# Layer 0 of a two-layer macaron block: where the side chains' matmuls may stand in the TensorE queue, and which engines do two of their elementwise steps

## The chip, the cores and the metric

The kernel runs on one core of a Trainium2 chip. A core has five engines that run side by side, each through its own queue in order: PE (TensorE, matmuls; its weight loads are shown as PEld), DVE (VectorE), ACT (ScalarE), POOL (GpSimd) and SP (SyncE, which here issues most DMAs). The metric is the device time of one execution in microseconds; the time before is a median of 3630.62 us over three runs (3627.19 to 3651.11).

## What is computed

The input x is 16 batches of 512 tokens of 128 channels. Two layers follow one another; each adds to x half of a feed-forward block, an attention, and half of the same feed-forward block again. The change touches layer 0 alone. Cut to that layer:

```python
def fp4_linear(x, w):                 # blocks of 16 along the last dimension
    return einsum('bsk,nk->bsn', fp4_quant_dequant(x), fp4_quant_dequant(w))

def L0_ffn(x, w_gate, w_up, w_down):  # 128 -> 352 -> 128
    h = silu(fp4_linear(x, w_gate)) * fp4_linear(x, w_up)
    return fp4_linear(h, w_down)

def L0_attn(x, ...):                  # 16 heads of 8 channels
    dist = clip(idx[None, :] - idx[:, None], -64, 64) + 64
    pe_k, pe_v = rel_emb_k[dist], rel_emb_v[dist]
    q, k, v = split(x @ W_qkv + b_qkv);  q = q / sqrt(8)
    score = einsum('bhqd,bhkd->bhqk', q, k) + einsum('bhqd,qkd->bhqk', q, pe_k)
    attn = softmax(score)
    ctx = einsum('bhqk,bhkd->bhqd', attn, v) + einsum('bhqk,qkd->bhqd', attn, pe_v)
    return ctx @ W_out + b_out

x = x + 0.5 * L0_ffn(layernorm(x), ...)
x = x + L0_attn(layernorm(x), ...)
x = x + 0.5 * L0_ffn(layernorm(x), ...)
```

Layer 1 has a linear attention and a feed-forward block with its own small attention and a mixture of experts; its code is the same before and after.

## The kernel before

Layer 0 works in units: one batch and one half of its queries (256 of 512), so 32 units. The code of a unit consists of several generators, and `interleave` (L446) steps them in turn, each by its own schedule: a generator gets a number of steps and a span of positions in units, and the one that is furthest behind its schedule makes its next step. The order in which instructions are written this way is called the order of emission here. It is a priority, not yet the order of execution: a scheduler places each instruction on its engine's queue at compile time, by its own estimate of when the operands and buffers are ready, and may place a later one first. `issue_after(ins)` around some instructions forbids that towards one instruction: those on the same engine as `ins` are queued behind it, without a wait.

The generators of the loop (`layer0`, L457) are:

- The stream of maxima (`maxima`, L332), for a later unit: 32 score groups. A score group (`scores`, L257) is four matmuls of 128 columns (L263) and, within the band of relative positions, eight of 64 (L267), into one PSUM bank of the pool `pS` ("sps", three banks). DVE takes the row maxima out of the bank (L341), and at the end the maxima are reduced (L347), transposed on PE (L349) and sent through DRAM into the operand BD.
- `main` (L358): the same 32 score groups again; ACT takes the exponentials out of the bank (L369). Behind each eight groups stand bursts of small matmuls (L272, L274) for attn times v ("av") and attn times the band table ("rps"). The band part is written to DRAM and read back as `cr`; av is copied to `cx` by ACT (L412).
- `fin` (L416): adds cr to cx on DVE (L422, two instructions), transposes cx (L430), divides by the sum (L433, L434), transposes (L437, copied out in L438) and multiplies by W_out (L440), and adds the result to x (L443). Its span is the stretch from 0.45 to 0.9 of the next unit.
- `prep` (L275) and `prepV` (L316): the layer norm and projection of a later batch (L282, L286, L305, L319).
- `head` and `tail`: `FFN.half` (L107) before and after the attention, for 256 tokens each. It normalizes, quantizes (`quant_steps`, L64, with POOL at L79 and L81), transposes (L115), makes "gate" (L121, tanh at L122, L123) and "up" (L125), multiplies both on DVE straight from PSUM (L126), quantizes the product h, transposes it (L133, copied in L135 and L136), multiplies by w_down (L139) and adds to x (L140). `head` loads x (L475) first; `tail` stores it last.

The matmuls of `fin`, `prep`, `prepV`, `head` and `tail` are called chain matmuls here. They share the PSUM pool `pM` ("mps") with two banks, and each bank is free again when the instruction that reads it out is done. `head` and `tail` share the pool `fk` with two buffers for each name; "q_y" is one of the names. Before the loop, head, prep and maxima of the first units are written out one after the other (L510 to L517): head(0), prep(0), maxima(0,0), then head(1), prep(1), 14 steps of the next maxima, and head(2).

The number of steps that each generator is given in `layer0` stands beside it: 33 per unit for the maxima, 59 for `main`, 5 for `fin`, 21 for `head` and `tail`, 11 for `prep`.

Of the kernel before, what the change touches and what calls it, by code (L numbers as in the profile page):

```python
# [25 lines left out]
class K:  # L26
# [23 lines left out]
    def ln_steps(s, xb, out, wk, n):  # L50

        nc=s.nc
        st=wk.tile([128,n,6],F32,name="ln_st"); mv=wk.tile([128,n,2],F32,name="ln_mv")
        for j in range(n):
            nc.vector.bn_stats(st[:,j,:],xb[:,j,:])  # L55
            nc.vector.bn_aggr(mv[:,j,:],st[:,j,:]); yield  # L56
        ve=wk.tile([128,n],F32,name="ln_ve"); rs=wk.tile([128,n],F32,name="ln_rs"); mr=wk.tile([128,n],F32,name="ln_mr")
        nc.vector.tensor_scalar(ve,mv[:,:,1],1e-5,None,ALU.add)  # L58
        nc.gpsimd.tensor_tensor(rs,ve,s.negh[:,:n],ALU.pow); yield  # L59
        nc.vector.scalar_tensor_tensor(mr,mv[:,:,0],-1.0,rs,ALU.mult,ALU.mult)  # L60
        for j in range(n):
            nc.scalar.activation(out[:,j,:],xb[:,j,:],AF.Identity,bias=mr[:,j:j+1],scale=rs[:,j:j+1])  # L62
        yield
    def quant_steps(s, X, wk, P, nb, tag):  # L64

        nc=s.nc
        n=nb*16
# [3 lines left out]
        nc.vector.tensor_scalar(sc[:P],sc[:P],float(np.float32(1/6)),1e-12,ALU.mult,ALU.max)  # L71
# [6 lines left out]
        nc.vector.scalar_tensor_tensor(y[:P],y[:P],SHRINK,M[:P],ALU.mult,ALU.add); yield  # L78
        nc.gpsimd.tensor_tensor(M[:P],y[:P],M[:P],ALU.subtract)  # L79
        M3=M.rearrange("p (b k) -> p b k",k=16)  # L80
        nc.gpsimd.tensor_tensor(M3[:P],M3[:P],sc[:P].unsqueeze(2).to_broadcast([P,nb,16]),ALU.mult)  # L81
        yield M

class FFN:
# [22 lines left out]
    def half(f, xb, half, wk, pp):  # L107

        s=f.s; nc=s.nc
        xh=xb[:,2*half:2*half+2,:]  # L110
        xn=wk.tile([128,2,128],F32,name="f_x")
        yield from s.ln_steps(xh,xn,wk,2)
        for xq in s.quant_steps(xn.rearrange("p a b -> p (a b)"),wk,128,16,"xq"): yield
        ps=pp.tile([128,512],F32,name="mps")
        for j in range(2): nc.tensor.transpose(ps[:,j*128:(j+1)*128],xq[:,j*128:(j+1)*128],s.ident)  # L115
        xqT=wk.tile([128,256],F32,name="f_x"); nc.scalar.copy(xqT,ps[:,:256]); yield
        h=wk.tile([128,2,I],F32,name="f_h")
        for j in range(2):
            t=h[:,j,:]
            g=pp.tile([128,512],F32,name="mps")  # L120
            nc.tensor.matmul(g[:,:I],xqT[:,j*128:(j+1)*128],f.wguT[:,0,:],start=True,stop=True)  # L121
# [3 lines left out]
            nc.tensor.matmul(u[:,:I],xqT[:,j*128:(j+1)*128],f.wguT[:,1,:],start=True,stop=True)  # L125
            nc.vector.scalar_tensor_tensor(t,u[:,:I],0.5,t,ALU.mult,ALU.mult); yield  # L126
        for hq in s.quant_steps(h.rearrange("p a b -> p (a b)"),wk,128,44,"hq"): yield
        hq=hq.rearrange("p (a b) -> p a b",a=2)
        for j in range(2):
            ps=pp.tile([128,512],F32,name="mps")  # L130
            for c in range(3):
                P=min(128,I-c*128)
                nc.tensor.transpose(ps[:P,c*128:(c+1)*128],hq[:,j,c*128:c*128+P],s.ident)  # L133
            hT=wk.tile([128,3,128],F32,name="hT",bufs=1)
            nc.scalar.copy(hT[:,0:2,:],ps[:,:256])  # L135
            nc.scalar.copy(hT[:96,2,:],ps[:96,256:384])  # L136
            for c in range(3):
                P=min(128,I-c*128)
# [7 lines left out]
class Attn0:  # L146
# [110 lines left out]
    def scores(a, out, kt, half, b, BD, TQ, KS):  # L257
# [2 lines left out]
        sd=a.side(kt,blk); ib=a.inband(kt,blk)  # L260
        o4=out.rearrange("p (x g c) -> p g x c",x=8,g=4)
        for g in range(4):
            nc.tensor.matmul(o4[:,g],KS[:,sd,g*512+kt*128:g*512+(kt+1)*128],BD[:,g,:,b*32:b*32+32].rearrange("p h (x j) -> p x h j",j=4),start=(g==0),stop=(not ib and g==3),skip_group_check=True)  # L263
        if ib:
            for x in range(8):
                w0=kt*128-blk*32-x+a.OFF
                nc.tensor.matmul(out[:,x*64:x*64+64],a.ET[:,w0:w0+128],TQ[:,:,b*32+4*x:b*32+4*x+4],start=False,stop=(x==7),skip_group_check=True)  # L267

    xnT={}; pend={}; last=None
    def run(a, mms):  # L270
# [4 lines left out]
    def prep(a, b, xb, wk, pM):  # L275
# [6 lines left out]
        for j in range(4): nc.tensor.transpose(ps[:,j*128:(j+1)*128],xn[:,j,:],a.ident)  # L282
        xnT=a.xnT[b]=wk.tile([128,512],F32,name="xnT",bufs=2); nc.scalar.copy(xnT,ps); yield
        for z in range(2):
            ps=pM.tile([128,512],F32,name="mps")
            nc.tensor.matmul(ps,a.w[:,z*128:(z+1)*128],xnT,start=True,stop=True)  # L286
# [18 lines left out]
        nc.tensor.matmul(ps[:32],a.eb.rearrange("p a b -> p (a b)"),q,start=True,stop=True)  # L305
# [26 lines left out]
    def maxima(a, b, half, wk, pS, pM):  # L332
# [16 lines left out]
        nc.tensor.transpose(ps[:,:128],mk.rearrange("p s b x -> p (s b x)"),a.ident)  # L349
# [66 lines left out]
    def fin(a, b, half, X, wk, pM):  # L416

        s=a.s; nc=a.nc; cx,cr=a.pend.pop((b,half)); xb=X[b]
        def add():
            for s2 in range(2):  # L420
                o=cx.rearrange("p z (b j s x) -> p s (z b) x j",j=4,s=2,x=4)[:,s2]
                nc.vector.tensor_tensor(o,o,cr.rearrange("p (x j z b s) -> p s (z b) x j",x=4,j=4,z=4,s=2)[:,s2],ALU.add)  # L422
        if a.last is None: add()
        else:
            with s.tc.issue_after(a.last): add()
        yield
        cn=wk.tile([128,2,128],F32,name="cn")
        for t in range(2):
            ps=pM.tile([128,512],F32,name="mps")
            for z in range(4): nc.tensor.transpose(ps[:,z*128:z*128+128],cx[:,z,t*128:t*128+128],a.ident)  # L430
# [6 lines left out]
        for t in range(2): nc.tensor.transpose(ps[:,t*128:t*128+128],cn[:,t,:],a.ident)  # L437
        ct=wk.tile([128,2,128],F32,name="cn").rearrange("p a b -> p (a b)"); nc.scalar.copy(ct,ps[:,:256])  # L438
        ps=pM.tile([128,512],F32,name="mps")
        for t in range(2): nc.tensor.matmul(ps[:,t*128:(t+1)*128],ct[:,t*128:(t+1)*128],a.wo,start=True,stop=True)  # L440
# [16 lines left out]
def layer0(tc, s, w, src, dst, nb=16):  # L457
# [3 lines left out]
    with ExitStack() as c:  # L461
# [576 lines left out]
```

## Time and profile before

| | |
|---|---|
| median of three runs | 3630.62 us |
| the profiled execution's own time | 3633.94 us |
| its span, first to last instruction | 3632.2 us |
| mean granted TensorE clock | 0.900 |
| PE busy | 2825.0 us, 78% of the span |
| PEld busy | 2032.3 us, 56% |
| DVE busy | 2444.9 us, 67% |
| ACT busy | 1693.8 us, 47% |
| POOL busy | 838.9 us, 23% |
| L341, maxima out of PSUM, x1024 | 702.5 us, 701 ns each |
| L369, exponentials out of PSUM, x1024 | 576.4 us, 599 ns each |
| L263, scores, x8192 | 736.4 us of PE |
| L267, band scores, x7168 | 370.3 us of PE |

The profile is of one execution, taken by the hardware. Busy time counts instructions, not queues; matmuls overlap, so a matmul's own duration (222 ns at L263) is longer than the distance to the next one. A wait is put down to whatever released it last by the profile. "<- issue" is a wait for nothing that the profile shows. L422 and the like are lines of the kernel above.

### The profile page before, as it was taken

Reading aid. Unit: us, or ns where it says so; the run is one execution under the profiler, and the core shown is the slowest. Engines: PE = TensorE matmul, PEld = TensorE weight load, DVE = VectorE, ACT = ScalarE, POOL = GpSimd, SP = SyncE. Lnnn points to the kernel's source line nnn. Section 1 sums busy time; section 2 is a strip of 40 time slices with the busy share of each in tenths; the row PEclk is TensorE's granted clock in tenths of the full one; section 3 lists DMA queues with packets and bytes.
Section 4 is the critical chain, followed back from the end, with each engine's and each line's share of the span. In section 5 each row is a group of like instructions: output and inputs, shape, how many; then the busy total and the mean of one; then the engine's idle time right before and its main releaser. Section 6 shows DMA issues by size and latency. Waiting matters only on the chain. (4 is left out here: it accounts for less than half of the span.)

```text
span 3632.2 us, 95259 instructions
## 1 busy us (share of the span) xinstructions
PE 2825.0 (78%) x40077; PEld 2032.3 (56%) x40077; DVE 2444.9 (67%) x6508; ACT 1693.8 (47%) x3391; POOL 838.9 (23%) x789
## 2 busy tenths in 40 slices
PE   5578989889898889888896388873788888878570
PEld 3357777667676677666775244431565555555230
DVE  5568788777887788877773467774546655655356
ACT  3145555545455454545554155533455454445242
POOL 4122222222222222222110222212112211111226
PEclk8799999999999999999998599886899989989785
DMA  3232222321223222222210111104312222121401
GB/s 105 54 91 71 57 53 59 81 63 52 65 65 77 64 50 58 76 74 62 53 33 19 32 33 36 36 33 123 90 54 73 59 63 56 36 62 36 126 17 46
DMA packets 290159, 217.23 MB, mean 60 GB/s; under 512 B 77402, under 2 KB 257476, under 8 KB 289604
## 3 DMA queue, kind: packets, MB, share of 16 engines
q1 hardware_dynamic: 284468, 207.72, 21.6%
q8 instruction: 315, 5.16, 0.6%
q10 hardware_dynamic: 5264, 3.43, 0.4%
q14 instruction: 112, 0.92, 0.1%
HBM read 110.28 MB, written 100.78 MB: 58 GB/s over the span
## 5 line engine op out<-in xcount | busy, mean ns | idle before, releaser
L341 DVE TRANSPOSE_TENSOR_REDUCE mx<-sps 128x16 f32<-128x512 f32 x1024 | 702.5, 701 | 261.7 <-PE sps L263 137.2
L263 PE MATMUL sps<-a_BD,a_KS 128*128 128x128 f16 x8192 | 736.4, 222 | 136.2 <-DVE mx L341 65.6
L369 ACT ACTIVATE PT<-sps 128x512 f32<-128x512 f32 x1024 | 576.4, 599 | 433.8 <-PE sps L267 238.1
L263 PEld LDWEIGHTS <-a_KS 128*128 128x128 f16 x8192 | 546.1, 98 | 296.4 <-issue 260.0
L59 POOL TENSOR_TENSOR ln_rs<-ln_ve,negh 128x4 f32<-128x4 f32 (+1 forms) x192 | 176.9, 930 | 855.1 <-DVE ln_ve L58 760.6
L267 PE MATMUL sps<-a_TQ,a_ET 128*128 128x64 f16 x7168 | 370.3, 195 | 0.0
L721 DVE SCALAR_TENSOR_TENSOR moe<-mps,oh,moe 128x128 f32<-128x128 f32 x896 | 289.8, 341 | 110.7 <-PE mps L719 96.5
L79 POOL TENSOR_TENSOR q_M<-q_y,q_M 128x704 f32<-128x704 f32 (+2 forms) x129 | 157.0, 1218 | 784.6 <-DVE q_y L78 658.6
L719 PE MATMUL mps<-f_W,T 128*128 128x512 f32 x512 | 297.1, 701 | 24.8 <-DVE moe L721 20.0
L267 PEld LDWEIGHTS <-a_ET 128*128 128x128 f16 x7168 | 311.2, 99 | 2.3 <-issue 1.9
L274 PE MATMUL av<-PT,a_V 128*32 128x256 f32 x3840 | 251.9, 387 | 0.0
L894 DVE TENSOR_TENSOR a_at<-pp,a_cm 128x1024 f32<-128x1024 f32 x128 | 154.3, 1214 | 79.6 <-PE pp L892 78.6
L892 PE MATMUL pp<-a_F 64*128 64x128 f32 x2048 | 169.8, 306 | 41.4 <-DVE a_at L894 30.2
L892 PEld LDWEIGHTS pp<-a_F 64*128 64x128 f32 x2048 | 143.3, 206 | 93.0 <-DVE a_at L894 36.9
L719 PEld LDWEIGHTS mps<-f_W,T 128*128 128x128 f32 x512 | 102.7, 222 | 125.0 <-issue 75.3
L274 PEld LDWEIGHTS av<-PT,a_V 128*32 128x32 f32 x3840 | 121.4, 111 | 68.7 <-issue 5.0
L874 ACT ACTIVATE a_F<-pp 128x1024 f32<-128x1024 f32 x128 | 127.0, 1025 | 46.8 <-PE pp L872 40.5
L62 ACT ACTIVATE xn<-xn,ln_mr,ln_rs 128x128 f32<-128x128 f32 x256 | 103.6, 481 | 95.5 <-DVE ln_mr L60 75.2
L274 PE MATMUL rps<-PT,a_TV 128*32 128x64 f32 x6912 | 134.5, 222 | 4.6 <-issue 4.4
L139 PE MATMUL mps<-wdT,hT 128*128 128x128 f32 (+1 forms) x768 | 126.9, 301 | 5.6 <-ACT hT L136 4.0
L673 ACT COPY f_PT<-St 32x512 f32<-32x512 f32 x128 | 78.7, 615 | 106.0 <-DVE St L672 99.9
L872 PE MATMUL pp<-a_QK,a_PK 128*128 128x512 f16 x256 | 82.7, 413 | 54.4 <-DMA a_QK<-a1d 26.6
(342 smaller groups left out, 5330.2 us busy)
## 6 DMA issues: line engine op xcount, KB each, us to landing
QM<-a_HM SPq DMA_DIRECT2D x180, 128.0 KB
a_TQ<-QM SPq DMA_DIRECT2D x120, 192.0 KB
RD<-RV SPq DMA_DIRECT2D x32, 512.0 KB
a_KS<-KSd SPq DMA_DIRECT2D x128, 96.0 KB
a_QK<-a1d SPq DMA_DIRECT2D x128, 96.0 KB
xn<-X SPq DMA_DIRECT2D x32, 256.0 KB
a1d<-a_hi SPq DMA_DIRECT2D x64, 128.0 KB
a_BD<-QS SPq DMA_DIRECT2D x128, 58.0 KB
```

The source lines that it names most:

```text
L59: nc.gpsimd.tensor_tensor(rs,ve,s.negh[:,:n],ALU.pow); yield
L79: nc.gpsimd.tensor_tensor(M[:P],y[:P],M[:P],ALU.subtract)
L263: nc.tensor.matmul(o4[:,g],KS[:,sd,g*512+kt*128:g*512+(kt+1)*128],BD[:,g,:,b*32:b*32+32].rearrange("p h (x j) -> p x h j",j=4),start=(g==0 ...
L267: nc.tensor.matmul(out[:,x*64:x*64+64],a.ET[:,w0:w0+128],TQ[:,:,b*32+4*x:b*32+4*x+4],start=False,stop=(x==7),skip_group_check=True)
L274: for p,q in mms[1:]: a.nc.tensor.matmul(*p,**q)
L341: with a.s.tc.high_priority(): r=nc.vector.tensor_reduce(mx[:,kt,:,bb],ps.rearrange("p (i c) -> p i c",c=32),axis=AX.X,op=ALU.max,apply_tr ...
L369: nc.scalar.activation(pt[:,:,bb*32:bb*32+32].rearrange("p h (x j) -> p x h j",j=4),ps.rearrange("p (x h j) -> p x h j",x=8,j=4),AF.Exp)
L719: nc.tensor.matmul(ps,yT[:,j*128:(j+1)*128],a.W[:,e2*4:e2*4+4,:],start=True,stop=True)
L721: nc.vector.scalar_tensor_tensor(moe[:,j,:],ps[:,e*128:(e+1)*128],oh[:,j,e2*4+e:e2*4+e+1],moe[:,j,:],ALU.mult,ALU.add)
L874: nc.scalar.activation(f,ps,AF.Relu)
L892: nc.tensor.matmul(ps[:,hh,bs],f[hh*64:hh*64+64,1,bs],f[hh*64:hh*64+64,0,bs],start=True,stop=True)
L894: nc.vector.tensor_tensor(k,ps.rearrange("p h (b q) -> p (h b) q",b=4),a.cm.unsqueeze(1).to_broadcast([128,8,128]),ALU.mult)
```

## The change

Four things are changed in layer 0, and nothing else:

1. `scores` notes its last matmul in `lastmm`. A helper `gate` puts chain matmuls, and the transpose of the maxima (L349), behind it with `issue_after`: each is queued on PE behind the last score group emitted before it. The matmuls of `prepV` and the bursts are not gated.
2. A step boundary (`yield`) is added between L347 and L349, between the copies of hT (L135, L136) and L139, and between L438 and L440. The numbers of steps are raised to match: 34, 6 and 23.
3. The product of h with "up" (L126) leaves DVE: ACT copies 0.5 times "up" out of PSUM into a buffer "q_y", and POOL multiplies.
4. The two additions of `fin` (L422) move from DVE to POOL, and lose their `issue_after` on the last maximum emitted.

```diff
+    lastmm=None
+    def gate(s):
+
+        return s.tc.issue_after(s.lastmm) if s.lastmm is not None else ExitStack()
...
-        for j in range(2): nc.tensor.transpose(ps[:,j*128:(j+1)*128],xq[:,j*128:(j+1)*128],s.ident)
+        with s.gate():
+            for j in range(2): nc.tensor.transpose(ps[:,j*128:(j+1)*128],xq[:,j*128:(j+1)*128],s.ident)
...
-            nc.tensor.matmul(u[:,:I],xqT[:,j*128:(j+1)*128],f.wguT[:,1,:],start=True,stop=True)
-            nc.vector.scalar_tensor_tensor(t,u[:,:I],0.5,t,ALU.mult,ALU.mult); yield
+            with s.gate(): nc.tensor.matmul(u[:,:I],xqT[:,j*128:(j+1)*128],f.wguT[:,1,:],start=True,stop=True)
+            v=wk.tile([128,704],F32,name="q_y")[:,:I]; nc.scalar.activation(v,u[:,:I],AF.Copy,scale=0.5); nc.gpsimd.tensor_tensor(t,t,v,ALU.mult); yield
...
-            nc.scalar.copy(hT[:96,2,:],ps[:96,256:384])
+            nc.scalar.copy(hT[:96,2,:],ps[:96,256:384]); yield
             for c in range(3):
                 P=min(128,I-c*128)
-                nc.tensor.matmul(ps[:,384:512],hT[:P,c,:],f.wdT[:P,c,:],start=(c==0),stop=(c==2),skip_group_check=True)
+                with s.gate(): nc.tensor.matmul(ps[:,384:512],hT[:P,c,:],f.wdT[:P,c,:],start=(c==0),stop=(c==2),skip_group_check=True)
...
+        a.s.lastmm=getattr(r,"ins",r)
...
+        yield
         ps=pS.tile([128,512],F32,name="sps")
-        nc.tensor.transpose(ps[:,:128],mk.rearrange("p s b x -> p (s b x)"),a.ident)
+        with a.s.gate(): nc.tensor.transpose(ps[:,:128],mk.rearrange("p s b x -> p (s b x)"),a.ident)
...
-                nc.vector.tensor_tensor(o,o,cr.rearrange("p (x j z b s) -> p s (z b) x j",x=4,j=4,z=4,s=2)[:,s2],ALU.add)
-        if a.last is None: add()
-        else:
-            with s.tc.issue_after(a.last): add()
+                nc.gpsimd.tensor_tensor(o,o,cr.rearrange("p (x j z b s) -> p s (z b) x j",x=4,j=4,z=4,s=2)[:,s2],ALU.add)
+        add()
...
-        ct=wk.tile([128,2,128],F32,name="cn").rearrange("p a b -> p (a b)"); nc.scalar.copy(ct,ps[:,:256])
+        ct=wk.tile([128,2,128],F32,name="cn").rearrange("p a b -> p (a b)"); nc.scalar.copy(ct,ps[:,:256]); yield
...
-        S=[(part(99999),33*2*nb,W['part'],2*nb+W['part'])]
+        S=[(part(99999),34*2*nb,W['part'],2*nb+W['part'])]
...
-                at(A.fin(b,h,X,wk,pM),5,1+fn[0],1+fn[1])
-                at(tail(b,h),21,1+fn[1]+.001,1+fn[1]+tl)
-                if b+hl<nb: at(head(b+hl,h),21,*W['head'])
+                at(A.fin(b,h,X,wk,pM),6,1+fn[0],1+fn[1])
+                at(tail(b,h),23,1+fn[1]+.001,1+fn[1]+tl)
+                if b+hl<nb: at(head(b+hl,h),23,*W['head'])
```

The same gate is put around L121, L133, L282, L286, L305, L430, L437 and L440.

More of the change, by code (lines that the diff above doesn't have):

```diff
@@ L120, in half @@
             g=pp.tile([128,512],F32,name="mps")
-            nc.tensor.matmul(g[:,:I],xqT[:,j*128:(j+1)*128],f.wguT[:,0,:],start=True,stop=True)
+            with s.gate(): nc.tensor.matmul(g[:,:I],xqT[:,j*128:(j+1)*128],f.wguT[:,0,:],start=True,stop=True)
             nc.scalar.activation(t,g[:,:I],AF.Tanh,scale=0.5)
@@ L130, in half @@
             ps=pp.tile([128,512],F32,name="mps")
+            with s.gate():
+                for c in range(3):
+                    P=min(128,I-c*128)
+                    nc.tensor.transpose(ps[:P,c*128:(c+1)*128],hq[:,j,c*128:c*128+P],s.ident)
+            hT=wk.tile([128,3,128],F32,name="hT",bufs=1)
+            nc.scalar.copy(hT[:,0:2,:],ps[:,:256])
+            nc.scalar.copy(hT[:96,2,:],ps[:96,256:384]); yield
             for c in range(3):
                 P=min(128,I-c*128)
[L133 to L139 removed]
+                with s.gate(): nc.tensor.matmul(ps[:,384:512],hT[:P,c,:],f.wdT[:P,c,:],start=(c==0),stop=(c==2),skip_group_check=True)
             nc.vector.scalar_tensor_tensor(xh[:,j,:],ps[:,384:512],0.5,xh[:,j,:],ALU.mult,ALU.add); yield
@@ L262, in scores @@
         for g in range(4):
-            nc.tensor.matmul(o4[:,g],KS[:,sd,g*512+kt*128:g*512+(kt+1)*128],BD[:,g,:,b*32:b*32+32].rearrange("p h (x j) -> p x h j",j=4),start=(g==0),stop=(not ib and g==3),skip_group_check=True)
+            r=nc.tensor.matmul(o4[:,g],KS[:,sd,g*512+kt*128:g*512+(kt+1)*128],BD[:,g,:,b*32:b*32+32].rearrange("p h (x j) -> p x h j",j=4),start=(g==0),stop=(not ib and g==3),skip_group_check=True)
         if ib:
@@ L266, in scores @@
                 w0=kt*128-blk*32-x+a.OFF
-                nc.tensor.matmul(out[:,x*64:x*64+64],a.ET[:,w0:w0+128],TQ[:,:,b*32+4*x:b*32+4*x+4],start=False,stop=(x==7),skip_group_check=True)
+                r=nc.tensor.matmul(out[:,x*64:x*64+64],a.ET[:,w0:w0+128],TQ[:,:,b*32+4*x:b*32+4*x+4],start=False,stop=(x==7),skip_group_check=True)
+        a.s.lastmm=getattr(r,"ins",r)
     xnT={}; pend={}; last=None
@@ L281, in prep @@
         ps=pM.tile([128,512],F32,name="mps")
-        for j in range(4): nc.tensor.transpose(ps[:,j*128:(j+1)*128],xn[:,j,:],a.ident)
+        with s.gate():
+            for j in range(4): nc.tensor.transpose(ps[:,j*128:(j+1)*128],xn[:,j,:],a.ident)
         xnT=a.xnT[b]=wk.tile([128,512],F32,name="xnT",bufs=2); nc.scalar.copy(xnT,ps); yield
@@ L285, in prep @@
             ps=pM.tile([128,512],F32,name="mps")
-            nc.tensor.matmul(ps,a.w[:,z*128:(z+1)*128],xnT,start=True,stop=True)
+            with s.gate(): nc.tensor.matmul(ps,a.w[:,z*128:(z+1)*128],xnT,start=True,stop=True)
             f=wk.tile([128,512],F32,name="qk0") if z==0 else wk.tile([128,4,128],F32,name="xn").rearrange("p a b -> p (a b)")
@@ L304, in prep @@
         ps=pM.tile([128,512],F32,name="mps")
-        nc.tensor.matmul(ps[:32],a.eb.rearrange("p a b -> p (a b)"),q,start=True,stop=True)
+        with s.gate(): nc.tensor.matmul(ps[:32],a.eb.rearrange("p a b -> p (a b)"),q,start=True,stop=True)
         rhi=wk.tile([128,512],F16,name="qkhi",bufs=2)[:32]; rlo=wk.tile([128,512],F16,name="qklo")[:32]
@@ L429, in fin @@
             ps=pM.tile([128,512],F32,name="mps")
-            for z in range(4): nc.tensor.transpose(ps[:,z*128:z*128+128],cx[:,z,t*128:t*128+128],a.ident)
+            with s.gate():
+                for z in range(4): nc.tensor.transpose(ps[:,z*128:z*128+128],cx[:,z,t*128:t*128+128],a.ident)
             p3=ps.rearrange("p (h c) -> p h c",c=32)
@@ L436, in fin @@
         ps=pM.tile([128,512],F32,name="mps")
-        for t in range(2): nc.tensor.transpose(ps[:,t*128:t*128+128],cn[:,t,:],a.ident)
-        ct=wk.tile([128,2,128],F32,name="cn").rearrange("p a b -> p (a b)"); nc.scalar.copy(ct,ps[:,:256])
+        with s.gate():
+            for t in range(2): nc.tensor.transpose(ps[:,t*128:t*128+128],cn[:,t,:],a.ident)
+        ct=wk.tile([128,2,128],F32,name="cn").rearrange("p a b -> p (a b)"); nc.scalar.copy(ct,ps[:,:256]); yield
         ps=pM.tile([128,512],F32,name="mps")
-        for t in range(2): nc.tensor.matmul(ps[:,t*128:(t+1)*128],ct[:,t*128:(t+1)*128],a.wo,start=True,stop=True)
+        with s.gate():
+            for t in range(2): nc.tensor.matmul(ps[:,t*128:(t+1)*128],ct[:,t*128:(t+1)*128],a.wo,start=True,stop=True)
         xh=xb[:,2*half:2*half+2,:]
```

## The prediction

> **What bounds the kernel now.** I read the page's busy shares first, then layer 0's steady stretch alone, since the change touches nothing else. Layer 0 lasts to about 2045 us; its loop over 32 units (one batch's half each) runs its scores from 125 to 1974 us, and from 300 to 1700 us it repeats.
>
> ```profile
> 300.00:1700.00 1400.00, 1242.94 (x22154) 981.36 (x22147) 1114.65 (x2502) 717.30 (x1585) 337.04 (x316) 0.98 0.25 64
> ```
>
> The columns are PE, PEld, DVE, ACT, POOL busy, then clock and DMA. L347 ran 48 times there, two per unit: 24 units of 58.3 us. DVE is busy 46.4 us of each, ACT 29.9, POOL 14.0. PE looks 89% busy, but matmuls overlap, so I took start-to-start distances from the trace. Dense, an L263 matmul starts 57 ns after the last, L267 28.5, L121 and L125 296, L133 109, L139 111. Adding these (a burst's distances as they are) gives 1121 us of unavoidable starts; the other 279 us of 1400 (11.6 us per unit) are PE waiting. So PE's order decides, and the question is what its head of queue waits for. The waits of the same stretch:
>
> ```profile
> DVE ln_st L55 <- DMA x<-in_L_attn_x_dram: 45.5, 11, 5.2
> PE sps L263 <- DVE mx L341: 44.5, 51, 3.9
> ...
> PEld mps L437 <- issue: 20.8, 11, 1.9
> ...
> PE mps L437 <- DVE a_V L321: 19.8, 12, 1.8
> ...
> PEld mps L440 <- ACT cn L438: 12.9, 9, 2.0
> ...
> PE sps L349 <- DVE hq_sc L71: 9.9, 11, 0.9
> ```
>
> (Columns: total us, times, longest.) Single chain matmuls stop PE for up to 2 us, with score groups standing ready behind them. L437's wait is for L321, which has nothing to do with its operand: L321 reads the PSUM bank ("mps" has two) that L437 will write. In the timeline:
>
> ```profile
> 856.23 1.39 POOL L81 TENSOR_TENSOR q_M<-q_M,hq_sc 128x704 f32<-128x704 f32 x1
> ...
> 856.67 0.98 DVE L71 TENSOR_SCALAR hq_sc<-hq_sc 128x44 f32<-128x44 f32 x1
> ...
> 857.58 1.01 DVE L321 TENSOR_TENSOR a_V<-mps,a_bev 128x384 f32<-128x384 f32 x2
> ...
> 858.73 0.30 PE L437 MATMUL mps<-ident,cn 128*128 128x128 f32 x1 [1.75 <-DVE a_V L321]
> ```
>
> PE stands from 857 to 858.73 because DVE reaches L321 late; a small instruction ahead of it, L71, took 0.98 us and ended with POOL's L81.
>
> Measured the same way, the waits ahead of chain matmuls sum to 115.2 us in the 24 units: L437 24.8, L349 20.0, L440 15.8, L139 14.1, L133 10.5, L430 10.3, L305 6.8, L121 6.2, L125 4.2, L319 2.5. Why are they at the head too early? I counted, by the interleaving in the code, how many score groups are emitted before each chain matmul, and from the trace how many ran before it. All of L115, L121, L125, L282, L286, L305 and L319 ran ahead of their place in emission (medians 12, 11, 6, 8, 4, 1 and 3 groups, a group lasting 0.9 us); about half of L437 (12 ahead), L440, L430, L133 and L139 did; L349 none. Those that ran ahead hold 54.8 us of the 115.2.
>
> **The change, part by part.**
>
> *The gate.* It forbids running ahead, so each hoisted matmul meets its operand and bank later by up to 12 groups (some 10 us) against waits of 2 us. I let two thirds of the 54.8 go: 36.5 us (ends: none, since a matmul can also meet a busier bank; all).
>
> *The added yields.* L349, L440 and the L139 matmuls get a step of other work between operand and use. Their not-hoisted waits are 20.0, 14.9 and 8.3 = 43.2 us; a step is one score group of the maxima stream (1.7 us) for L349, against 0.8 us per wait, and about 4.4 us (0.45 of a unit over 6) for L440, against 2. I take four fifths: 34.6 us. Splitting L139 from L133 holds a bank one step longer (2.5 us, 58.3/23): four halves of it are 10 us more per unit on bank holds that I sum from first write to last read to 61 of 2x58.3 us. That still leaves idle bank time, so I charge nothing; without that cover, see the second rival.
>
> Together 71.1 us in 24 units, 3.0 per unit; the loop has 30.4 such units, so 90 us (ends 0 and 115.2/24x30.4 = 146). What is late next are the scores' own banks: waits ahead of L263 are 133 of the 279 us, 48%. I give a quarter of the 90 back (between none and half): 68 us.
>
> *Off DVE, onto ACT and POOL.*
>
> ```profile
> L422 DVE TENSOR_TENSOR cx<-cx,a_cr 128x512 f32<-128x512 f32 x48 | 50.6, 1104 | 0.0
> L126 DVE SCALAR_TENSOR_TENSOR f_h<-mps,f_h 128x352 f32<-128x352 f32 x97 | 48.8, 503 | 1.3 <-PE mps L125 1.3
> ```
>
> DVE loses 2x1.104 + 4x0.503 = 4.2 us per unit. ACT gains four copies of 128x352 from PSUM at L122's 0.47 (same shape): 1.9 us, on 29.9 of 58.3. PE waits only 22.8 us in 24 units for L369's bank; 6% more of that is 2 us over the loop. POOL gains four 128x352 products and two 512-wide additions:
>
> ```profile
> L79 POOL TENSOR_TENSOR q_M<-q_y,q_M 128x704 f32<-128x704 f32 x58 | 98.2, 1693 | 571.3 <-DVE q_y L78 461.2 <-PE sps L263 68.7 <-PE mps L430 20.4
> L81 POOL TENSOR_TENSOR q_M<-q_M,hq_sc 128x704 f32<-128x704 f32 x58 | 86.3, 1488 | 3.4
> L79 POOL TENSOR_TENSOR q_M<-q_y,q_M 128x256 f32<-128x256 f32 x57 | 41.4, 727 | 142.9 <-DVE q_y L78 130.9 <-PE sps L263 10.2 <-DMA a_BD<-QS 1.4
> ...
> L298 POOL COPY a_HM<-qklo 128x512 f16<-128x512 f16 x14 | 24.7, 1764 | 0.9
> ```
>
> Between the 256 and 704 wide rows, 352 comes to 0.8 to 0.93; I take 0.85, 3.4 us. A contiguous 512-wide POOL operation takes 1.22 us (L764), a strided copy L298 1.76; the addition is strided on all sides, so 1.8 each (bounds 1.2 to 2.5), 3.6 us. POOL goes from 14.0 to 21 of 58.3 us: room enough. It is in order, and what queues behind a waiting addition is L59 and L79/L81, on which L62 and L133 wait. L422 waited on its DMA only twice (20.7 us, both at the end of layer 0), so that wait is charged there.
>
> Not all 4.2 us are saved: DVE lengthens beside POOL. Summing each DVE instruction's time above 1.08 times its own lower quartile, I get 55 us beside 337 us of POOL work, 0.16 per us, so 7.0 us more POOL cost DVE 1.1. DVE goes to about 43.3 us per unit. Its PE share: 20 us of PE's gaps lie beside L126 and L422, 19 of them at chain matmuls and so counted above. I add 10 us, and take off 5 for the new hand-over (L70 now waits for POOL where it followed L126 on its own engine): 5 net, ends -40 and +25.
>
> The Trainium skill (SBUF — State Buffer, "SBUF: two separate sides") speaks against this part: DVE and GpSimd share one port pair as an exclusive lock, held for a whole instruction, which bars DVE instructions with two SBUF inputs or in a two-port mode. The trace agrees in kind: L71 on hq_sc takes 131 ns at least, 176 in the median, 989 at most. Were DVE barred for all 7.0 us, the 4.2 saved would become 2.8 lost per unit, 85 us of DVE over the loop instead of a saving.
>
> *Ends.* Head(1), prep(1) and head(2) now follow the scores emitted before them; in the trace L115 of head(1) starts at 91 us, in the lull before the first score at 125 us. Against that, maxima(0,0) (125 to 163 us, DVE fully busy from 140 to 160) loses their DVE work. I let these cancel, -10 to +20. The last chain pays two products' hand-over (0.47+0.85-0.50 each) and 1.4 for the additions: 3 us, and the first halves 2. Cost 5.
>
> Sum: 68 + 5 - 2 - 5 = 66 us. The profiled execution took 3633.94 us (span 3632.2 and 1.7 around it): 3568; it lies 3.3 above the median of 3630.62, so 3565.
>
> **The rivals.**
>
> *Everything goes well:* all 146 us of chain waits go, none returns, and DVE's 25 show: 3634-146-25+7-3 = 3467. For it: waits of 2 us against 10 us of room. Against: PE is only one of two engines near 80%. Chance 0.12.
>
> *Slower: the input tile's chain.* Eleven times DVE waits for x (4.1 us each, L55 above): the last tail stores its X, only then is the buffer free, x loaded, and DVE stands in order; PE stops up to 3.9 us, and the clock then shows 0.5 for 3.4 to 6.8 us. The gate delays tails: the last L139 there ran 2 groups ahead, in the other unit of each pair 9 late. If it also gets 9 late and L55 keeps its place, some 5 us more wait and 2.5 us of half clock, 7.5x11 = 83 us, while half the gain stays: 3634+83-34-3 = 3680. It decides from 6 us per case. Against: only three groups of delay are forced, and L55 is placed anew. Chance 0.22.
>
> *The waits only move* to L263, because banks, not order, limit, or because half the chain was never hoisted: 3634-5+7-3 = 3633. For it: the 60 us of waits on matmuls that did not run ahead. Chance 0.16.
>
> **How the numbers follow.** The forecast itself has 0.50. One per cent, 36 us, is about what a measurement of this kernel tells from no change; below 3594 lie the forecast and the first rival, 0.62; within 0.16; above 0.22. The range, 3462 to 3682, reaches from the first rival's end to the slower rival and leaves out about 0.2.
>
> **What would show it.** Right: in 300 to 1700 us the waits of L437, L440 and L349 fall below 20 us together, L121 and L125 run at or after emission, more than 25 units fit, DVE's idle time ahead of L55 stays near 4 us each. Wrong: L263's waits for L341 or L369 grow by as much; DVE waits for POOL ahead of L70 or L58 for more than 1 us per unit; the addition takes over 2.5 us; PE stands ahead of L430 for POOL.

## Result, and the profile after

The changed kernel takes 3914.62 us (median of four, 3909.64 to 3926.01) against 3632.09 us: a ratio of 1.0772, 95% interval [1.0726, 1.0817], 282 us slower. The forecast of 3565 us, its range and the chance of 0.62 for "faster" were wrong. Layer 1 is untouched: from layer 0's last w_down matmul to the end it is 1588 us in both profiles.

From the page after (span 3915.0 us): the busy shares, then four of the costliest groups (busy, mean ns of one, idle time ahead of them and what ended it).

```profile
PE 2868.0 (73%) x40077; PEld 2064.5 (53%) x40077; DVE 2345.6 (60%) x6316; ACT 1758.7 (45%) x3519; POOL 1085.2 (28%) x981
...
L269 PE MATMUL sps<-a_BD,a_KS 128*128 128x128 f16 x8192 | 756.7, 224 | 393.6 <-DVE ln_mv L56 152.3
...
L432 POOL TENSOR_TENSOR cx<-cx,a_cr 128x512 f32<-128x512 f32 x64 | 128.0, 2034 | 583.2 <-DMA a_cr<-RD 578.9
...
L131 POOL TENSOR_TENSOR f_h<-f_h,q_y 128x352 f32<-128x352 f32 x128 | 120.8, 944 | 470.9 <-ACT q_y L131 413.6
...
L55 DVE BATCH_NORM_STATS2 ln_st<-x 128x6 f32<-128x128 f32 x192 | 46.3, 269 | 212.9 <-DMA x<-in_L_attn_x_dram 212.6
```

PE, DVE and ACT are all less busy than before in share: nothing has become the bound. The scores (L269, L263 before) wait for a layer-norm statistic, L56, which has nothing to do with scores. The same stretch as in the prediction, 300 to 1700 us, in windows (PE, PEld, DVE, ACT, POOL busy, clock, DMA):

```profile
300.00:1700.00 1400.00, 1090.49 (x19179) 863.26 (x19179) 886.95 (x2024) 654.30 (x1434) 445.68 (x393) 0.90 0.22 55
```

The DVE did 2024 instructions there where it did 2502, and the granted clock fell from 0.98 to 0.90. The waits of that stretch (total us, times, longest):

```profile
POOL cx L432 <- DMA a_cr<-RD: 416.6, 21, 29.4
...
DVE ln_st L55 <- DMA x<-in_L_attn_x_dram: 194.0, 10, 20.6
...
PE sps L269 <- DVE ln_mv L56: 133.9, 7, 20.4
...
PE sps L359 <- DVE mk L356: 5.4, 8, 0.7
```

Two stands of about 20 us each (a stand here: an engine does nothing because the instruction at the head of its queue waits): DVE at L55, for the input tile x, and POOL at the addition, for the band part a_cr. L359 (L349 before) has 5.4 us in its row. Time per unit, counted by the 32 exponentials of each, shows where the loss lies: from unit 8 on, before took 58, 59, 58, 58, 57, 60 us; after took 77, 57, 78, 55, 78, 55. Every second unit, the one in which a new x is loaded, costs 20 us more; the others are 2 to 5 us shorter.

One such stand, in the timeline of the kernel after (start, length, engine; in brackets the idle time ahead and its releaser):

```profile
1123.36 3.73 SPq L339 DMA_DIRECT2D a_TQ<-QM  x1
1127.35 0.29 DVE L146 SCALAR_TENSOR_TENSOR x<-mps,x 128x128 f32<-128x128 f32 x1 [1.39 <-PE mps L145]
...
1127.96 3.51 SPq L339 DMA_DIRECT2D a_TQ<-QM  x1
...
1131.57 0.72 SPq L416 DMA_DIRECT2D RD<-RV  x1
...
1141.35 1.36 SPq L419 DMA_DIRECT2D a_cr<-RD  x4
1142.81 0.39 SPq L497 DMA_DIRECT2D X<-x  x1
1145.23 3.92 POOL L432 TENSOR_TENSOR cx<-cx,a_cr 128x512 f32<-128x512 f32 x2 [28.39 <-DMA a_cr<-RD]
1145.26 0.39 SPq L486 DMA_DIRECT2D x<-in_L_attn_x_dram  x1
1148.26 0.87 DVE L55 BATCH_NORM_STATS2 ln_st<-x 128x6 f32<-128x128 f32 x4 [18.23 <-DMA x<-in_L_attn_x_dram]
1149.06 1.05 POOL L59 TENSOR_TENSOR ln_rs<-ln_ve,negh 128x4 f32<-128x4 f32 x1
1149.87 0.58 PE L269 MATMUL sps<-a_BD,a_KS 128*128 128x128 f16 x4 [17.98 <-DVE ln_mv L56]
```

The tail's last addition (L146) ends at 1127.6. SP is issuing the operand loads of the next maxima then (a TQ load holds its queue for 3.5 us), goes on to RD, and waits 9.1 us for RD to land before it reads it back. Only then comes the store of X; the load of x waits for that store, since x takes its buffer, and x is there at 1148.26. DVE, in order, stands at L55 for 18.23 us; the score banks fill, and PE and ACT stand with it. In the kernel before, the same queue of SP in its timeline:

```profile
756.29 0.39 SPq L486 DMA_DIRECT2D X<-x  x1
760.14 0.39 SPq L475 DMA_DIRECT2D x<-in_L_attn_x_dram  x1
760.64 1.68 SPq L315 DMA_DIRECT2D a_KS<-KSd  x4
762.36 0.26 SPq L329 DMA_DIRECT2D a_BD<-QS  x1
762.72 1.17 SPq L330 DMA_DIRECT2D a_TQ<-QM  x1
```

There store and load stood ahead of those loads and of RD, and DVE's wait was 5.2 us at most.

After a stand the clock is down: the window from 1150 to 1157 us was granted 0.64 (1.00 from 1100 to 1129). The Trainium skill (TensorE: Matmul & The Clock Gate, "What's actually happening") says that an idle window of about 3.4 us halves the clock until PE has been busy for about as long again; 0.64 over 7 us is 5 us at half speed, which agrees in kind and is somewhat longer.

Behind POOL's addition stands L59, without which no layer norm goes on. It was ready only with x here, so the second stand lies hidden under the first. The experiments ask whether either is enough alone.

### The profile page after: what moved, and what is told of

It is laid out like the page before. It is cut to its first block, busy times and chain, and to the rows that moved or that the text cites. A ratio compares the mean times of both kernels' runs of the same rounds, so it can differ in the third digit from the quotient of the medians.

```text
span 3915.0 us, 95479 instructions
## 1 busy us (share of the span) xinstructions
PE 2868.0 (73%) x40077; PEld 2064.5 (53%) x40077; DVE 2345.6 (60%) x6316; ACT 1758.7 (45%) x3519; POOL 1085.2 (28%) x981
## 5 line engine op out<-in xcount | busy, mean ns | idle before, releaser
L269 PE MATMUL sps<-a_BD,a_KS 128*128 128x128 f16 x8192 | 756.7, 224 | 393.6 <-DVE ln_mv L56 152.3
L269 PEld LDWEIGHTS <-a_KS 128*128 128x128 f16 x8192 | 561.0, 99 | 554.3 <-issue 511.8
L59 POOL TENSOR_TENSOR ln_rs<-ln_ve,negh 128x4 f32<-128x4 f32 (+1 forms) x192 | 176.5, 928 | 527.3 <-DVE ln_ve L58 499.8
L432 POOL TENSOR_TENSOR cx<-cx,a_cr 128x512 f32<-128x512 f32 x64 | 128.0, 2034 | 583.2 <-DMA a_cr<-RD 578.9
L83 POOL TENSOR_TENSOR q_M<-q_y,q_M 128x704 f32<-128x704 f32 (+2 forms) x129 | 165.1, 1284 | 380.4 <-DVE q_y L82 257.4
L282 PE MATMUL av<-PT,a_V 128*32 128x256 f32 x3840 | 266.3, 403 | 0.0
L131 POOL TENSOR_TENSOR f_h<-f_h,q_y 128x352 f32<-128x352 f32 x128 | 120.8, 944 | 470.9 <-ACT q_y L131 413.6
L905 DVE TENSOR_TENSOR a_at<-pp,a_cm 128x1024 f32<-128x1024 f32 x128 | 154.2, 1215 | 72.4 <-PE pp L903 71.9
L55 DVE BATCH_NORM_STATS2 ln_st<-x 128x6 f32<-128x128 f32 x192 | 46.3, 269 | 212.9 <-DMA x<-in_L_attn_x_dram 212.6
L282 PEld LDWEIGHTS av<-PT,a_V 128*32 128x32 f32 x3840 | 125.0, 115 | 76.5 <-issue 17.2
L62 ACT ACTIVATE xn<-x,ln_mr,ln_rs 128x128 f32<-128x128 f32 x64 | 26.4, 482 | 266.3 <-DVE ln_mr L60 266.3
```

Of the source, the lines that this page charges most:

```text
L269: r=nc.tensor.matmul(o4[:,g],KS[:,sd,g*512+kt*128:g*512+(kt+1)*128],BD[:,g,:,b*32:b*32+32].rearrange("p h (x j) -> p x h j",j=4),start=(g= ...
L282: for p,q in mms[1:]: a.nc.tensor.matmul(*p,**q)
L905: nc.vector.tensor_tensor(k,ps.rearrange("p h (b q) -> p (h b) q",b=4),a.cm.unsqueeze(1).to_broadcast([128,8,128]),ALU.mult)
```

## Experiments

All ratios are against the kernel before on the same chip. "L55" is DVE's wait for x at L55, "ln_mr" DVE's wait at L60 for POOL's L59, "a_cr" POOL's wait for the addition's operand (lines of before), each from 400 to 1900 us, in total us and times, from the waits of each profile (0 where the profile shows none); "per unit" is the mean of units 2 to 25 by their exponentials. The kernel before took 3621 to 3651 us on these chips, so rows are compared by their ratios.

| run | us | ratio | L55 | ln_mr | a_cr | per unit |
|---|---|---|---|---|---|---|
| before | 3632.09 | 1 | 45.5/11 | 0.8/3 | 0 | 57.8 |
| after | 3914.62 | 1.0772 [1.0726, 1.0817] | 212.6/11 | 8.3/11 | 442.3/23 | 66.8 |
| no_gate | 4096.36 | 1.1232 [1.1211, 1.1252] | 112.7/10 | 107.7/10 | 267.1/20 | 75.0 |
| gate_yield | 3904.60 | 1.0697 [1.0679, 1.0715] | 217.6/11 | 5.6/11 | 0 | 67.3 |
| gate_only | 3894.05 | 1.0670 [1.0644, 1.0696] | 196.6/11 | 0 | 0 | 67.0 |
| yield_only | 3842.64 | 1.0604 [1.0587, 1.0622] | 218.4/11 | 5.8/12 | 0 | 66.6 |
| y139 | 3735.79 | 1.0232 [1.0208, 1.0256] | 99.4/11 | 2.0/12 | 0 | 61.9 |
| pool_only | 3999.57 | 1.1038 [1.0988, 1.1087] | 80.0/11 | 174.8/43 | 289.2/16 | 71.0 |
| add_back | 3875.86 | 1.0693 [1.0643, 1.0743] | 207.5/11 | 5.1/10 | 0 | 66.3 |
| after_xh | 4064.89 | 1.1136 [1.1111, 1.1161] | 284.7/21 | 12.6/20 | 252.1/17 | 72.4 |
| before_xh | 3920.40 | 1.0743 [1.0726, 1.0760] | 272.3/21 | 10.7/13 | 0 | 69.7 |
| actq_add | 3828.68 | 1.0555 [1.0511, 1.0600] | 73.2/11 | 4.8/10 | 0 | 64.4 |
| after_g55 | 3951.38 | 1.0912 [1.0894, 1.0931] | 0 | 225.3/35 | 347.2/20 | 67.5 |
| before_g55 | 3635.83 | 1.0030 [1.0018, 1.0042] | 0 | 7.0/16 | 0 | 57.0 |
| g55_add | 3664.35 | 1.0106 [1.0074, 1.0138] | 0 | 11.5/23 | 0 | 57.5 |
| g55_padd | 3641.07 | 1.0046 [1.0026, 1.0066] | 0 | 11.8/24 | 129.1/15 | 56.3 |
| before_g55_loop | 3653.47 | 1.0008 [0.9992, 1.0025] | 0 | 7.7/15 | 0 | 57.6 |
| padd_loop | 3646.51 | 0.9987 [0.9971, 1.0003] | 0 | 11.5/23 | 122.2/14 | 57.0 |
| padd_mix | 3646.24 | 0.9982 [0.9970, 0.9993] | 0 | 11.5/23 | 77.7/11 | 57.3 |
| padd_25 | 3622.27 | 0.9921 [0.9905, 0.9936] | 0 | 11.5/23 | 113.2/14 | 57.0 |

### One part at a time

no_gate is the change with the gate returning nothing:

```diff
-        return s.tc.issue_after(s.lastmm) if s.lastmm is not None else ExitStack()
+        return ExitStack()
```

> The changed kernel with the gate taken out (added steps, product and addition on GpSimd stay). Theory 1: the gate makes each tail end late, its store of X stands on SP behind the wait for RD, the load of x behind it, and DVE stands at L55 (11 times 19 us, before 4). Without the gate the tails end early again: L55 waits under 80 us in all, 3600 to 3680. Theory 2: GpSimd in order is the cause, the addition waiting for a_cr with the quantization behind it: still 3800 or more. Theory 3: the gate costs by holding chain matmuls behind scores that wait for banks, x or not: 3600 to 3680 as well, so this run doesn't tell 1 from 3.

gate_yield keeps gate and steps; product and addition are back on DVE:

```diff
-            v=wk.tile([128,704],F32,name="q_y")[:,:I]; nc.scalar.activation(v,u[:,:I],AF.Copy,scale=0.5); nc.gpsimd.tensor_tensor(t,t,v,ALU.mult); yield
+            nc.vector.scalar_tensor_tensor(t,u[:,:I],0.5,t,ALU.mult,ALU.mult); yield
...
-                nc.gpsimd.tensor_tensor(o,o,cr.rearrange("p (x j z b s) -> p s (z b) x j",x=4,j=4,z=4,s=2)[:,s2],ALU.add)
-        add()
+                nc.vector.tensor_tensor(o,o,cr.rearrange("p (x j z b s) -> p s (z b) x j",x=4,j=4,z=4,s=2)[:,s2],ALU.add)
+        if a.last is None: add()
+        else:
+            with s.tc.issue_after(a.last): add()
```

> The gate and the added steps alone; product and addition are back on DVE as before the change. Theory 1 and 3: the loss stays, 3800 or more, L55 waiting over 150 us in all. Theory 2: the loss is gone, 3600 to 3680.

pool_only is the opposite: before with this diff the other way round, and nothing else.

> The kernel before with product and addition on GpSimd, up copied by ScalarE, alone (no gate, no added steps). Theory 1: 3600 to 3670 with L55 under 80 us. Theory 2 (the addition waits for a_cr at the head of GpSimd's queue, L59 and the quantization behind it): 3800 or more, DVE or PE waiting on what stands behind the addition.

yield_only is before with the three added steps and their numbers (34, 6, 23) alone:

> The kernel before with the added steps and their numbers alone (no gate, product and addition on DVE). Theory 1: the tails end where they did, L55 waits under 80 us in 400 to 1900 us, 3600 to 3670. If any shift of the order makes x late, L55 waits over 150 us and it takes 3800 or more.

gate_only is before with the gate alone, and y139 is before with one of the three steps alone, the one ahead of L139 (numbers 23):

```diff
-            nc.scalar.copy(hT[:96,2,:],ps[:96,256:384])
+            nc.scalar.copy(hT[:96,2,:],ps[:96,256:384]); yield
```

> The kernel before with the gate alone (no added steps, product and addition on DVE). If the gate makes tails late as well: L55 over 150 us, 3800 or more. If it leaves x where it was: the chain waits of PE (4.8 us per unit before) fall, and against that its start is longer by some 40 us: 3580 to 3680.

> The kernel before with only the step between the copies of hT and L139 (and 23 steps for head and tail). Theory 1: this step makes the tail's last L140 and so the store of X late, past RD on SP; it is enough by itself: L55 over 150 us in 400 to 1900 us, 3780 to 3860. If the steps at L349 and L440 do it: 3600 to 3650.

Each of the three parts alone is 6 to 10% slower, so the losses don't add: gate alone (1.0670) and steps alone (1.0604) each bring DVE's stand at L55, 18 to 20 us eleven times, and one step boundary brings half of it (9 us each). The moves to POOL alone are the worst (1.1038), with another stand: DVE at L60 for POOL's L59, behind an addition that waits for its DMA. In the queue of SP both gate_only and yield_only have X's store behind the TQ loads and RD, and x's load behind the wait for RD, as after has.

Without the gate the change is slower still (1.1232), where 3600 to 3680 us and an L55 under 80 us were expected, so the gate is not what loses most. In no_gate the stands come in turn and not one under the other: both units of each pair are long (69 and 80 us from unit 8 on, where before has 58 and 59), and PE waits as well for a quantizing product of POOL that is queued behind a waiting addition:

```profile
PE mps L120 <- POOL q_M L85: 102.8, 10, 11.8
```

These rows show where no_gate and pool_only stand; their losses were not added up from them.

### The two stands taken away

add_back is after with only the addition back on DVE (second half of gate_yield's diff):

> The changed kernel with only the addition back on DVE; x is loaded as in the change. Theory 1 with 2: L55 still waits some 9 us per unit, since the store of X still stands behind RD and a_cr: 3850 to 3930, and nothing gained. Theory 2 alone: 3600 to 3700.

POOL then waits for no a_cr, and 1.0693 remains: L55's stand is enough without POOL's.

after_xh and before_xh load x in ten half tiles, each by its own head, so that a load waits for a store made a unit earlier:

```diff
-        xk=c.enter_context(tc.tile_pool(name="xk",bufs=5))
+        xk=c.enter_context(tc.tile_pool(name="xk",bufs=10))
...
-            t=xk.tile([128,4,128],F32,name="x"); X[b]=t
-            nc.sync.dma_start(t,tok(src,b))
+            t=xk.tile([128,2,128],F32,name="x"); X[b][h]=t
+            nc.sync.dma_start(t,tok(src,b)[:,2*h:2*h+2,:])
```

> The changed kernel with x in ten half tiles instead of five whole ones (the same memory): a half is free one unit earlier, so its load no longer waits for the store that DVE's L55 stands behind. Theory 1: L55's wait falls from 213 us in 400 to 1900 us to under 20; 11 times (19.3 less 4.1) is 167 us, and half clock after 11 long stops some 50 more: about 3690. Theory 2 and 3: 3850 or more, the wait comes back at POOL or at the scores.

> The kernel before with x in ten half tiles. Theory 1: its 11 stops of PE of 3.9 us and some 2.5 us of half clock after each go: about 3560. If the stop is filled by something else that is late at the same place: 3610 to 3640.

A miss: DVE stood 21 times instead of 11, and x was late for L55 again. In SP's timeline of before_xh x's load stands once behind the wait for RD (issued at 941.8 us) and once behind four TQ loads (at 1014.7). The edit made the kernel before, with nothing of the change in it, 7.4% slower, as much as the change does: a kernel can lose as much by the place of L55 in DVE's queue against that of x's load in SP's, without any of the change's operations.

actq_add is add_back with X's store and x's load issued from ACT's queue:

```diff
-            nc.sync.dma_start(t,tok(src,b))
+            nc.scalar.dma_start(t,tok(src,b))
...
-            nc.sync.dma_start(tok(dst,b)[:,2*h:2*h+2,:],X[b][:,2*h:2*h+2,:])
+            nc.scalar.dma_start(tok(dst,b)[:,2*h:2*h+2,:],X[b][:,2*h:2*h+2,:])
```

> add_back with the store of X and the load of x issued from ACT's DMA queue and not from SP's, five whole tiles of x as in the change. Theory 1 (SP's order makes x late, not the store's or the load's own time): L55's wait falls from 19 us to at most 5 each, 3600 to 3720. If the tails are late of themselves: L55 still waits over 10 us each, 3800 or more.

L55's stand falls from 18.9 to 6.7 us each, and 47 us come back against add_back: SP's queue made most of x's lateness. The time, 3828.68 us, is still over both 3720 and 3800, though L55 no longer waits 10 us: 5.5% remain. ACT, which now issues store and load in order, stands some 7 us twice in each pair of units, once ahead of the store (the row names a TQ load as what ended it) and once ahead of the load, for the store. That this is the rest of the loss was not shown by a run. The waits:

```profile
ACT PT L379 <- DMA a_TQ<-QM: 80.3, 12, 7.7
...
ACT PT L379 <- DMA X<-x: 76.4, 11, 7.9
...
DVE ln_st L55 <- DMA x<-in_L_attn_x_dram: 73.2, 11, 7.7
```

The Trainium skill (DMA: Bandwidth & Descriptors, "Issuing engines are not separate DMA queues") says that issuing from several engines saves only the sequencer's time of issuing, usually small beside the DMA. Here what it saved isn't small: SP's queue stood 3.5 us for one TQ load and 9.1 us in waiting for RD, and x, which had been behind them, came 12 us sooner for L55 from another queue (18.9 less 6.7).

after_g55 takes the first stand away in two steps: the half tiles are loaded by the head before, and the head's L55 is queued on DVE behind the last maximum emitted. before_g55 is the same edit on before:

```diff
+            with (s.tc.issue_after(s.lastmax) if late and s.lastmax is not None else ExitStack()): nc.vector.bn_stats(st[:,j,:],xb[:,j,:])
...
-            if b<nb: xload(b); yield from F.half(X[b],h,fk,pF)
+            if b<nb: xload(b,h); xload(*((b,1) if h==0 else (b+1,0))); yield from F.half(X[b],h,fk,pF,True)
```

> The changed kernel, x in ten half tiles, each loaded by the head before the one that uses it, and the head's first statistics (L55) queued on DVE behind the last maximum emitted, so that DVE can't come to L55 early. In the changed kernel DVE stands at L55 9.2 us per unit of 65.2 (before 1.7 of 57.7): the difference, 7.5, is the whole loss. Theory 1 (that stand is the cause): under 1 us per unit at L55, 7.5 x 30.4 = 228 us come back, and some of the half clock: 3630 to 3690. Theory 3 (any wait removed turns up at the scores' banks, order is not the limit): 3850 or more with L55 under 1 us per unit.

> The kernel before with the same three edits to x. Theory 1: the 1.7 us per unit at L55 go, 52 us, and half clock after them: 3540 to 3600. Theory 3: 3630 or slower although L55 waits under 1 us per unit.

On before it gains nothing (1.0030), though the 45.5 us of waits at L55 are gone: a miss of its own, since 3540 to 3600 us were expected. On after, L55 no longer waits, yet the kernel is slower than after, where 3630 to 3690 us were expected: the second stand comes out from under the first, which g55_add and g55_padd below test. The waits of after_g55:

```profile
POOL cx L433 <- DMA a_cr<-RD: 347.2, 20, 29.9
...
DVE ln_mr L61 <- POOL ln_rs L60: 225.3, 35, 20.1
...
PE sps L270 <- DVE ln_mr L61: 211.8, 11, 19.9
```

Read from the bottom: PE waits for DVE's L61, which waits for POOL's L60, which is queued behind the addition, which waits for the DMA. g55_add puts the addition back on DVE; g55_padd leaves it on POOL and orders it behind the last POOL instruction of the side chains emitted (L59 or L81 of before):

```diff
-        add()
+        with s.pgate(): add()
...
+    def pgate(s): return s.tc.issue_after(s.lastpool) if s.lastpool is not None else ExitStack()
```

> after_g55 with the addition back on DVE, behind the last maximum as before the change. In after_g55 L55 no longer waits, and DVE stands the same 20 us, eleven times, at ln_mr (L60 in the changed kernel, L61 there), because ln_rs stands on GpSimd behind the addition that waits for a_cr. Theory 1 with 2 (the loss is two engines in order, each able to stand at something that SP brings some 20 us late; either alone is enough): both waits under 1 us per unit, 3600 to 3690. Theory 3: a third stand of the same size turns up, 3850 or more.

> after_g55 with the addition kept on GpSimd, but queued behind the last GpSimd instruction of the side chains emitted before it, as DVE's was behind the last maximum. Theory 2: GpSimd waits for a_cr under 2 us per unit, DVE at ln_mr under 1, 3600 to 3690. If the work on GpSimd itself costs (shared with DVE, slower): no wait for a_cr and still over 3750.

With both stands gone from DVE and PE the ratio falls from 1.0772 to 1.0106 and 1.0046. The loss is these two stands; gate, steps, ACT's copy and POOL's two operations are all still in g55_padd. POOL itself still waits 129.1 us for a_cr there, 4.9 us per unit where under 2 were expected, but DVE's wait behind it is down from 225.3 to 11.8 us.

### Why it is no faster even then

Of what was left, the start looked like one part: the first two units took 173.6 and 177.5 us in before_g55 and g55_padd against 130.5 in before. padd_loop and before_g55_loop apply the orders only inside the loop:

```diff
-        interleave(*S)
+        s.on=True; interleave(*S); s.on=False
```

> g55_padd with its three orders imposed only inside the loop, not on what is written out ahead of it. If the start is what it lost: the first 128 exponentials take 235 to 255 us and not 277, and the time falls by 25 to 45 us to 3595 to 3615, faster than before. If the loop itself costs: 3630 to 3650 again.

> before_g55 with L55's order imposed only inside the loop. If the start is what it lost: 3590 to 3612; if not, 3625 to 3645.

The first two units are 132.1 and 127.1 us again, and unit 2 starts 22 and 25 us sooner. But the 25 to 45 us expected did not come back: units 2 to 25 grew by 15 to 17 us (from 1351.2 to 1367.7 and from 1367.7 to 1382.7), and layer 0 ends only 2.5 and 10 us sooner. So the start was mostly not a loss, only time spent earlier.

The two kernels differ now by the change and by the addition's order on POOL. By stretches, the exponentials of units 2 to 25 take 1367.7 us in padd_loop and 1382.7 in before_g55_loop: the change does gain 15 us. Units 26 and 27 take 120.3 against 105.6 and give it back. At that place in padd_loop's timeline:

```profile
1699.24 3.93 POOL L436 TENSOR_TENSOR cx<-cx,a_cr 128x512 f32<-128x512 f32 x2 [14.69 <-DMA a_cr<-RD]
1703.06 0.67 POOL L89 TENSOR_TENSOR q_M<-q_M,xq_sc 128x256 f32<-128x256 f32 x1
...
1703.79 0.69 PE L124 MATMUL mps<-ident,q_M 128*128 128x128 f32 x2 [10.99 <-POOL q_M L89]
```

The additions of unit 25 stand on POOL between the two products of the last head's quantizer; a gated transpose (L124) waits for the second with the scores behind it. padd_25 puts the additions of that unit alone on DVE, behind the last maximum emitted; padd_mix does so for unit 25 and all later ones:

```diff
-                nc.gpsimd.tensor_tensor(o,o,cr.rearrange("p (x j z b s) -> p s (z b) x j",x=4,j=4,z=4,s=2)[:,s2],ALU.add)
+                (nc.vector if dv else nc.gpsimd).tensor_tensor(o,o,cr.rearrange("p (x j z b s) -> p s (z b) x j",x=4,j=4,z=4,s=2)[:,s2],ALU.add)
...
+        dv=2*b+half==25
```

> The change with both stands out of the way, orders inside the loop only, as in padd_loop, but the additions of unit 25 alone are back on DVE behind the last maximum emitted. Theory: in padd_loop the middle 24 units (from the exponentials of unit 2 to those of unit 26) took 15 us less than in before_g55_loop (1367.7 against 1382.7), and units 26 and 27 gave 15 us back (120.3 against 105.6), because a gated transpose of the last head stood 11 us for POOL's quantizing product, queued behind the additions of unit 25, which waited 15 us for their DMA. Then units 26 and 27 take 105 to 110 us here, PE's wait of 11 us for that product is gone, and the ratio is 0.995 to 0.998. Rival: the 15 us are the price of the fuller POOL and ACT queues at the end and stay: units 26 and 27 take 116 us or more and the ratio is that of padd_loop, 0.9987.

> As padd_25, but the additions of every unit from 25 on are on DVE (behind the last maximum as long as there is one). First theory: as padd_25, and the last four units, which took 179.7 us in padd_loop against 175.8 in before_g55_loop, come to 176 to 178: ratio 0.994 to 0.998. Rival: late additions on DVE meet the last tails, which are DVE's, and the last four units take 180 us or more: no better than padd_25.

padd_25 takes 110.0 us for units 26 and 27, the wait of 11 us is gone, and it is faster than before: 0.9921 [0.9905, 0.9936], more than the 0.995 to 0.998 expected. Of those 27 us its profile shows 17 in layer 0, which ends at 2028 us against 2044 in before; the rest can't be placed, since before was profiled on another chip and layer 1, whose code is the same, took 1578 to 1604 us in the twenty profiles. So half a per cent is the sure part of it. In padd_mix the rival was right: with all late additions on DVE the last four units take 186.9 us (176.9 in padd_25), and most of the gain is gone. Two of padd_25's lines from its page, and its stretch from 300 to 1700 us:

```profile
PE 2834.6 (78%) x40077; PEld 2044.7 (56%) x40077; DVE 2338.4 (65%) x6318; ACT 1750.1 (48%) x3519; POOL 1088.4 (30%) x979
...
L436 POOL TENSOR_TENSOR cx<-cx,a_cr 128x512 f32<-128x512 f32 x62 | 127.0, 2078 | 134.1 <-DMA a_cr<-RD 134.1
```

```profile
300.00:1700.00 1400.00, 1262.92 (x22606) 1004.18 (x22603) 1043.82 (x2385) 765.95 (x1696) 530.96 (x462) 0.98 0.26 65
```

DVE has less to do than before (2338 against 2445 us), POOL waits 134 us for a_cr instead of 579, and the clock is at 0.98 again.

## Why the prediction was wrong, and where it was right

**The gate and the steps took away the three waits they were aimed at, but less of all chain waits than forecast.** The waits of L437, L440 and L349 were to fall below 20 us in 24 units, 0.83 per unit. A wait is counted here as the excess of a start-to-start distance over the lower quartile of its line's distances, where that is over 0.1 us. From 300 to 1700 us the three fell from 2.47 to 0.78 us per unit, and in padd_25 to 0.99. But where x and the addition are out of the way, all chain waits from 400 to 1900 us went from 4.7 us per unit (before_g55_loop) to 3.5 (padd_25): 1.3 us, where 3.0 were forecast. Other cut-offs (0.02 to 0.15 us) and stretches give 1.3 to 2.0.

**The step that failed is the slower rival's "against": "only three groups of delay are forced, and L55 is placed anew".** By that argument the sum charged nothing for x; the rival had a chance of 0.22 and a price of 7.5 us a case. Its mechanism is what happened: X's store, then x's load, then DVE in order. But the delay of the tail was followed on PE only. It also carried X's store past the BD and TQ loads and RD in SP's queue, and L55 was not placed later to match: the waits for x rose by (212.6-45.5)/11 = 15.2 us a case, and two units (one case) by 2x(66.8-57.8) = 18 us with the clock. gate_only and yield_only show that either edit does it; y139, that a single step does half. Of the 283 us that layer 0 grew, units 2 to 25 hold 217, units 26 and 27 33, the last four 21 and the start 14.

**The second step that failed is POOL's: "L422 waited on its DMA only twice … so that wait is charged there".** On DVE L422 was ordered behind the last maximum. Without an order the addition stood at the head of POOL's queue, 21 times for 20 us, with L59 behind it, as the text itself had named. In the total of after it shows little (add_back 1.0693 against 1.0772), because it lies under the first stand. By itself it is 310 us: after_g55's 3951.38 against g55_padd's 3641.07, which differ in the addition's order alone.

**Sizes.** The product took 0.944 us (0.85 taken), the addition 2.03 (1.8; bounds 1.2 to 2.5). In padd_25's per-unit figures DVE has 3.3 us less (1174.08/26.0 = 45.2 against 1102.81/26.3 = 41.9 us, from 400 to 1900 us), as forecast (46.4 to 43.3), POOL 7.5 more (7.0). So DVE was not barred for POOL's whole time, which by the prediction's sum would have made it 2.8 us more.

**What goes back to L263** was set at a quarter. Between before_g55_loop and padd_25 the scores' own waits, counted in the same way, rose from 5.4 to 6.6 us per unit: 1.2 of the 1.3 saved (by the other cut-offs and stretches, half of it to all). This is the third rival, "the waits only move". It leaves little of the change when nothing stands: the clean gain is 15 us in 24 units, 0.6 us per unit, where 68 us over 30.4 units, 2.2 per unit, were forecast for gate and steps alone. Even without the stands the forecast of 3565 would have been too low: 0.9921 of 3632 is 3603. Of the signs named, it was DVE's idle time ahead of L55 that told: 19.4 us each where near 4 was asked, and 20.75 units fit from 300 to 1700 us instead of over 25. DVE's wait for POOL's product, 24.2 us in the 22.5 units from 400 to 1900 us, lies just over its mark of 1 us per unit.

**Ends.** Head and prep gated ahead of the loop were to cancel, -10 to +20: by the start of unit 2 it is +14 us (the first exponential 13 us earlier, the first two units 27 us longer).

Not shown: why the scheduler puts x's load and the addition where it does. Its estimates were not seen; only the orders they led to.

## What to carry to other kernels

When a step is moved, follow every DMA that hangs on it through its issuing queue, and ask which in-order engine has an instruction waiting at the end: here some 20 us on SP cost four engines as much. A wait that is short in a profile may be short only because of an order that the change removes, so price an instruction with a DMA operand at the head of the new engine's queue, with all that is queued behind. And two stands can hide each other: before giving a loss to one, remove it and see whether the other comes out.

## What the runs showed of the hardware

- One TQ load holds SP's queue for 3.3 to 3.7 us in many cases (49 of 120 after, 35 of 120 before; medians 2.8 and 0.87 us, 8.5 at most), as long as five maxima on DVE.
- From the store of RD to the first read back of it SP waited 9.1 us in the case shown (after, 400 to 1900 us: 111.2 us in 22 waits, 9.7 at most); all that is queued behind on SP waits too.
- The strided addition of 128x512 floats takes 2.03 us on POOL and 1.10 on DVE; POOL's contiguous 512-wide L764 took 1.27.
